# Linear attention and a top-2 mixture of experts on one core: fixed experts for each region's last rows, one plan for the rest, and output layers between the halves of the next first layers

## The chip, the cores and the metric

The kernel runs on one core of one Trainium2 chip. The metric is the device time of one execution in microseconds (us), without a profile; the median of three runs is taken. The kernel before took 337.9 us (337.5 to 340.69). A profile was recorded in a further execution.

## The reference

Two stages, each with a residual around it and a layer norm (without gain and bias) in front of it. B = 4 batches of 512 tokens of 256 numbers, all float32.

```python
# attention
q = k = x @ Wqk + bqk;  v = silu(x @ Wv + bv);  u = silu(x @ Wu + bu)
q = elu(heads(q)); kh = elu(heads(k)); vh = heads(v)      # 16 heads of 16
kv = einsum('bhnd,bhne->bhde', kh, vh)
out = einsum('bhnd,bhde->bhne', q, kv)
out = u * layernorm(out, ln_g, ln_b)
x = x + out @ Wo + bo
# experts: 8 of them, 256 -> 512 -> 256, the best two of each token
w, i = top_k(xn @ gate, 2); w = softmax(w)
h = silu(xn @ w0[e]) * (xn @ w1[e])
x = x + sum over the two of  w * (h @ wo[e])
```

The experts are computed here for the chosen tokens alone: 2048 tokens x 2 are 4096 rows, and each expert gets as many as chose it.

## The kernel before

**Rows by expert.** Each expert has a region of 2176 rows in a DRAM tensor xg. When a batch's gates are known, each token's two rows (the normed features, the weight and the token's number) are scattered into the regions of its two experts, behind the rows that are there already; POOL issues these scatters (L454). A block is 128 rows of one region, so one expert, and 32 to 39 blocks hold all rows, since a region's last block may be partly filled. Such a block's missing rows are written as padding (pads(), L462 to 469): rows of weight 0 with the numbers of spare tokens, 128 rows behind each region's end, eight DMAs of 130 KB on SP's queue.

**Planning.** Which regions the blocks lie in is known only at run time. plan(n, b) finds the first n blocks not yet taken: a matmul of ones with the counts (tot, L476) gives each region's end, some twenty small DVE operations on one partition (L483 to L539) turn this into a table with a first row and an expert's place in the weights for each block, and engines read the entries into registers (read(), L544). There are three plans: one for 9 blocks when the first two batches are scattered (EARLY), one for 16 more that are surely full when all four are (SURE - EARLY), and one for the last 14, of which 11 are usual (USUAL - SURE) and three come in a conditional part for unusual inputs. The last plan counts partly filled blocks too, and takes down where the padding starts.

**A block** goes through four steps, each in a function, and advance() moves a chain of blocks on by one step:
- fetch(): SP reads the first row and loads 128 rows of xg into g (L559; eight buffers, each free again when its block's add has landed).
- turn(): PE transposes g (gp, L570), ACT copies it out (L573), and ACT and DVE copy the expert's w0 and w1 (128x1024) from the resident weights to a staging place, found by the register (L579).
- hidden(): two times 16 matmuls, hp, one half for w0 and one for w1 (L590; each float32 matmul shows as two instructions), Silu of the first half on ACT (s, L596), the product on DVE (it, L598).
- finish(): four matmuls of it with the third weight (eo, L607), times the row's weight on DVE (ys, L612), and an indirect DMA on POOL that adds the rows to their tokens (L616).

The chain is such that PE's order is: transposes of block n+1, both halves of block n, eo of block n-1.

**Where the adds go.** The early blocks and those of the last plan add into a DRAM tensor y, which also has attention's result. The 16 surely full blocks are held back to the end: before their first add, y is copied to the output, and they add into the output. Adds into y are declared free of each other; adds into the output are not.

**Order.** Attention runs as four generators, one per batch, of 15 steps, started 4 steps apart; the loop's index is called at. The early plan is made at at = 19, the early blocks enter one per step from 20 on, so that the eighth enters at 27, the last index. Behind the loop come the two late plans, then the ninth early block, then the padding with the first block of the last plan, and the rest. This is the program's order; a planner in the compiler orders the instructions of each engine by it and by the times that it assumes, so that neighbours may be mixed. Each engine then executes in its own order. PSUM has eight buffers of one bank under one tag. In the page's names, blocks of the last plan end in r (g_0r, hp_0r); the names without r are early and held blocks.

Of the kernel before, what the change touches and what calls it, by code (L numbers as in the profile page):

```python
# [21 lines left out]
P = 128  # L22
# [7 lines left out]
def kernel(  # L30
# [35 lines left out]
    HPC = P // HEAD_DIM  # L66
    T = B * N
    TOPK = 2
    BLOCKS = T * TOPK // P + NE - 1
    USUAL = T * TOPK // P + NE // 2  # L70
    EARLY = 2 * N * TOPK // P - NE + 1
    SURE = T * TOPK // P - NE + 1
    REG = T + P
# [119 lines left out]
    ordinal = counting("ordinal", [1, BLOCKS, NE], [[1, BLOCKS], [0, NE]])  # L193
    rows = counting("rows", [1, BLOCKS], [[P, BLOCKS]])
# [3 lines left out]
    nc.gpsimd.memset(done, 0.0)  # L198
    empty = const.tile([P, ROW], F32, name="empty")
    nc.gpsimd.memset(empty, 0.0)  # L200
    nc.gpsimd.tensor_copy(empty[:, E + 1 : E + 2].bitcast(I32), spare_i)
# [255 lines left out]
                    bounds_check=NE * REG - 1, oob_is_err=True,  # L457
                ), b)

    def pads():  # L460

        loads, starts = nc.values_load_multi_w_load_instructions(  # L462
            state["pads"], engines=[mybir.EngineType.SP], min_val=0, max_val=NE * REG,
            skip_runtime_bounds_check_because="a region's start and a count",
        )
        for ins in loads:
            tc.keep_in_program_order(ins)
        for row in starts:
            apart(nc.sync.dma_start(out=xg[bass.ds(row, P), :], in_=empty), B - 1)

    def plan(n, b, last=False):

        tot = psum.tile([P, NE], F32, tag="a", name=f"tot_{b}_{last}")
        nc.tensor.matmul(tot, lhsT=ones, rhs=state["count"], start=True, stop=True)  # L476
        vec = [1, NE]

        def tmp(shape, what):
            return small.tile(shape, F32, tag=what, name=f"{what}_{b}_{last}", bufs=1)  # L480
# [13 lines left out]
        new = tmp(vec, "new")  # L494
        nc.vector.tensor_reduce(new, over, AX.X, ALU.add)
        nc.vector.tensor_tensor(new, new, done, ALU.subtract)
# [11 lines left out]
        nc.vector.tensor_tensor(base, done, cumex, ALU.subtract)  # L508
        nc.vector.scalar_tensor_tensor(base, base, float(P), region[0:1], ALU.mult, ALU.add)
# [19 lines left out]
        table = const.tile([1, 2, n], I32, name=f"table_{b}_{last}")  # L529
        nc.vector.tensor_scalar(table[:, 0, :], first, float(NE * REG), None, ALU.min)  # L530
        nc.vector.tensor_scalar(table[:, 1, :], which, float(NE - 1), float(OW), ALU.min, ALU.mult)
        if last:
            state["rest"] = const.tile([1, 1], I32, name="rest")
            nc.vector.tensor_copy(state["rest"], cum[:, NE - 1 : NE])
        else:
            taken = tmp(vec, "taken")
            nc.vector.tensor_scalar(taken, cumex, -1.0, float(n), ALU.mult, ALU.add)
            nc.vector.scalar_tensor_tensor(taken, taken, 0.0, new, ALU.max, ALU.min)
            nc.vector.tensor_tensor(done, done, taken, ALU.add)  # L539
        return [(f"{b}_{j}{'r' if last else ''}", b, table[0:1, :, j : j + 1]) for j in range(n)]  # L540

    def read(entry, most, *engines):

# [7 lines left out]

    def fetch(block):

        j, b, entry = block
        if j == f"{B - 1}_0r":
            pads()
        row = read(entry[:, 0, :], NE * REG, mybir.EngineType.SP)
        g = blk.tile([P, ROW], F32, tag="g", name=f"g_{j}", bufs=8)
        ins = nc.sync.dma_start(out=g, in_=xg[bass.ds(row, P), :])  # L559
        tc.declare_no_dep(ins.ins, group=f"after {b}", reason="rows of batches up to b")  # L560
        tc.add_to_no_dep_group("reads", ins.ins)
        return block, g

    def turn(block, g):


        j, b, entry = block
        ps = psum.tile([P, EC, P], F32, tag="a", name=f"gp_{j}")
        for c in range(EC):
            nc.tensor.transpose(ps[:, c, :], g[:, bass.ts(c, P)], ident)  # L570
# [3 lines left out]
        at = read(entry[:, 1, :], (NE - 1) * OW, mybir.EngineType.Activation, mybir.EngineType.DVE)  # L574
        w = []
        for i, copy in enumerate((nc.scalar.copy, nc.vector.tensor_copy)):
            w.append(staging[state["staged"] % 4])
            state["staged"] += 1
            copy(w[i], hw_sb[i][:, bass.ds(at, OW)])  # L579
        return block, w, g, gT  # L580

    def hidden(block, w, g, gT):

        j = block[0]
        both = []
        for i in range(2):
            ps = psum.tile([P, MC, P], F32, tag="a", name=f"hp_{j}_{i}")
            for m in range(MC):
                for k in range(EC):
                    nc.tensor.matmul(  # L590
                        ps[:, m, :], lhsT=w[i][:, bass.ds(k * M + m * P, P)],
                        rhs=gT[:, k, :], start=(k == 0), stop=(k == EC - 1),
                    )
            both.append(ps)
        s = work.tile([P, MC, P], F32, tag="s", name=f"s_{j}")
        nc.scalar.activation(s, both[0], AF.Silu)  # L596
        it = work.tile([P, MC, P], F32, tag="ex", name=f"it_{j}", bufs=4)
        nc.vector.tensor_tensor(it, s, both[1], ALU.mult)  # L598
        return block, g, it

    def finish(block, g, it):

        j, b, entry = block
        at = read(entry[:, 1, :], (NE - 1) * OW, mybir.EngineType.PE)
# [23 lines left out]
    def advance(block=None):  # L628
# [18 lines left out]
    for at in range(max(begin) + STAGES + 1):  # L647
# [4 lines left out]
            load_w2()  # L652

        if at == begin[1] + STAGES:
            ready += [None] * 1 + plan(EARLY, 1)
        if ready:
            block = ready.pop(0)
            if block:
                advance(block)

    held += plan(SURE - EARLY, B - 1)
    rest = plan(BLOCKS - SURE, B - 1, last=True)
    ready += rest[: USUAL - SURE]
    rare = rest[USUAL - SURE :]
    for block in ready + held:
        advance(block)
    while fetched or turned or made:
        advance()
    many = read(state["rest"], BLOCKS, *ENGINES)
    with tc.If(many > USUAL - (BLOCKS - len(rest))):  # L670
# [59 lines left out]
```

## Time and profile before

| what | us |
|---|---|
| median of three runs (lowest, highest) | 337.9 (337.5, 340.69) |
| the profiled execution, its own time | 345.68 |
| its span, first to last instruction | 343.6 |
| PE busy in the span | 305.5 |
| DVE, ACT, POOL busy | 162.7, 135.4, 118.4 |

The profile is of another execution than the three timed ones, and a longer one; a sum made from its rows belongs to its own 345.68 us. PE is TensorE's matmuls, PEld its weight loads, DVE the vector engine, ACT the scalar engine, POOL GpSimd, SP the engine whose queue loads most data. A line such as "PE hp L590 <- DVE arena L579: 2.0, 1, 2.0" says that PE, before an instruction of line 590 that writes hp, sat idle until DVE's line 579 was done, 2.0 us in all, one time, 2.0 us the longest. A timeline row gives the start, the duration, engine, line and operation, and in brackets the idle time of the engine before it. A "q" behind an engine (SPq) is its queue or sequencer.

Costs of single operations that the change touches:

| operation | duration of one, us | count |
|---|---|---|
| staging copy of w0 on ACT, L579 | 1.046 | 36 |
| staging copy of w1 on DVE, L579 | 0.693 | 36 |
| product it on DVE, L598 | 0.688 | 36 |
| Silu on ACT, L596 | 0.597 | 36 |
| ys on DVE, L612 | 0.482 | 36 |
| small operations of a plan on DVE | 0.13 to 0.28 | 20 each |
| add into the output on POOL, L616 | 1.602 | 16 |

### The profile page before, as it was taken

To read this page: it belongs to the slowest core of one execution; us is meant where nothing else is said; L and a number is where in the kernel's file an instruction comes from. 1 tells how busy PE (TensorE), PEld (TensorE's weight loads), DVE (VectorE), ACT (ScalarE), POOL (GpSimd) and SP (SyncE) were. 2 spreads that over 40 slices of the span, in tenths; PEclk is the share of its full clock that TensorE was granted. 3 is DMA by queue.
4 is the path that set the end of the run, shared out by engine and by line. 5 is a ranking of instruction groups with operands and counts; after the bars stand their busy time and mean duration, and the time that the engine had idled before them with its cause. 6 is when DMAs were issued, how large, how long until landed. Compare 5 with 4: busy or idle time off the path is not lost. (4 is left out here: it accounts for less than half of the span.)

```text
span 343.6 us, 6125 instructions
## 1 busy us (share of the span) xinstructions
PE 305.5 (89%) x2070; PEld 272.5 (79%) x2070; DVE 162.7 (47%) x556; ACT 135.4 (39%) x204; POOL 118.4 (34%) x147
## 2 busy tenths in 40 slices
PE   0999899899966898999789999999999999999950
PEld 0567686786866797998779999999999999999940
DVE  4756879686684764341823324232323324232210
ACT  1546728636524065531324243333424243333300
POOL 5420311317146076266324242333402333332321
PEclk9999999999995799999999999999999999999995
DMA  7999112044274542223552322323291433322121
GB/s 208 357 388 384 55 61 65 1 128 166 77 229 153 153 161 55 41 62 91 143 109 49 52 47 44 61 49 46 49 275 17 63 51 60 60 34 31 17 32 15
DMA packets 27871, 35.58 MB, mean 104 GB/s; under 512 B 2848, under 2 KB 22688, under 8 KB 27808
## 3 DMA queue, kind: packets, MB, share of 16 engines
q1 hardware_dynamic: 18960, 22.00, 20.4%
q0 software_dynamic: 6768, 11.08, 17.7%
q10 hardware_dynamic: 2112, 2.10, 1.9%
q8 instruction: 18, 0.29, 0.4%
q14 instruction: 13, 0.11, 0.1%
HBM read 22.89 MB, written 14.37 MB: 108 GB/s over the span
## 5 line engine op out<-in xcount | busy, mean ns | idle before, releaser
L590 PE MATMUL hp<-arena 128*128 128x128 f32 x800 | 94.5, 275 | 5.0 <-DVE arena L579 2.0
L590 PEld LDWEIGHTS hp<-arena 128*128 128x128 f32 x800 | 91.9, 192 | 5.7 <-issue 3.9
L598 DVE TENSOR_TENSOR it<-s,hp 128x512 f32<-128x512 f32 x25 | 17.2, 688 | 66.9 <-PE hp L590 51.1
L607 PE MATMUL eo<-arena,it 128*128 x200 | 47.5, 380 | 0.7 <-issue 0.7
L616 POOL DMA_INDIRECT out_dram<-ys,g x16 | 25.6, 1602 | 58.1 <-DVE ys L612 21.3
L454 POOL DMA_INDIRECT xg<-hn,idx_i x32 | 32.4, 1012 | 26.5 <-DVE mv L219 10.8
L607 PEld LDWEIGHTS eo<-arena,it 128*128 128x128 f32 x200 | 36.1, 190 | 5.0 <-issue 1.2
L579 ACT COPY arena<-w_sb 128x1024 f32 x36 | 37.6, 1046 | 4.0 <-DVE mv L219 1.3
L573 ACT COPY arena<-gp 128x256 f32<-128x256 f32 x25 | 9.3, 372 | 73.1 <-PE gp L570 65.7
L616 POOL DMA_INDIRECT y<-ys,g x9 | 15.3, 1702 | 29.9 <-DVE ys L612 13.8
L579 DVE COPY arena<-w_sb 128x1024 f32 x36 | 24.9, 693 | 1.3 <-DVE ys L612 0.7
L262 POOL TENSOR_TENSOR x<-x,bo 128x256 f32<-128x256 f32 x16 | 12.3, 794 | 37.7 <-DVE arena L245 29.1
L612 DVE TENSOR_SCALAR ys<-eo,g 128x256 f32<-128x256 f32 x25 | 12.0, 482 | 23.1 <-PE eo L607 20.6
L369 PE MATMUL ap<-wo,arena 128*128 128x256 f32 x64 | 17.2, 427 | 5.2 <-DVE first_False L526 2.8
L369 PEld LDWEIGHTS ap<-wo,arena 128*128 128x128 f32 x64 | 13.4, 216 | 8.3 <-issue 4.5
L596 ACT ACTIVATE s<-hp 128x512 f32<-128x512 f32 x25 | 14.9, 597 | 11.2 <-PE hp L590 9.5
L274 PE MATMUL qp<-arena,wqk 128*128 128x512 f32 x32 | 16.0, 647 | 0.2 <-ACT arena L267 0.2
L218 DVE BATCH_NORM_STATS2 st<-x 128x6 f32<-128x256 f32 x32 | 12.5, 416 | 4.5 <-DMA x<-in_x_dram 4.5
L292 PE MATMUL vp<-wv,arena 128*128 128x256 f32 x64 | 14.5, 379 | 0.0
L306 PE MATMUL up<-arena,wu 128*128 128x512 f32 x32 | 14.4, 592 | 0.0
L292 PEld LDWEIGHTS vp<-wv,arena 128*128 128x128 f32 x64 | 12.0, 190 | 2.4 <-issue 0.7
L253 PE MATMUL xTp<-ident,arena 128*128 128x128 f32 x32 | 5.2, 311 | 9.1 <-DVE arena L245 9.1
(269 smaller groups left out, 472.0 us busy)
## 6 DMA issues: line engine op xcount, KB each, us to landing
w_sb<-in_w_dram SPq DMA_DIRECT2D x16, 512.0 KB
arena<-in_w_dram SPq DMA_DIRECT2D x8, 512.0 KB
g<-xg SPq DMA_DIRECT2D x25, 130.0 KB
x<-in_x_dram SPq DMA_DIRECT2D x4, 512.0 KB
y<-x ACTq DMA_DIRECT2D x4, 512.0 KB
xg<-empty SPq DMA_DIRECT2D x9, 130.0 KB
xg<-hn,idx_i POOLq DMA_INDIRECT x32
wqk<-in_wqk_dram SPq DMA_DIRECT2D x1, 256.0 KB
```

Source lines behind the costliest of these rows:

```text
L218: nc.vector.bn_stats(out=st, in_=src[:, t, :])
L274: nc.tensor.matmul(ps, lhsT=wqk_sb[:, k, bass.ts(c, P)], rhs=xT[:, k, :], start=(k == 0), stop=(k == EC - 1),)
L292: nc.tensor.matmul(ps[:, t - t0, :], lhsT=xT[:, k, bass.ts(t, P)], rhs=wv_sb[:, k, :], start=(k == 0), stop=(k == EC - 1),)
L306: nc.tensor.matmul(ps, lhsT=wu_sb[:, k, bass.ts(c, P)], rhs=xT[:, k, :], start=(k == 0), stop=(k == EC - 1),)
L369: nc.tensor.matmul(ps[:, t - t0, :], lhsT=yT[:, c, bass.ts(t, P)], rhs=wo_sb[:, c, :], start=(c == 0), stop=(c == EC - 1),)
L454: apart(nc.gpsimd.indirect_dma_start(out=xg[:, :], out_offset=bass.IndirectOffsetOnAxis(ap=idx_i[:, t, k : k + 1], axis=0), in_=hn[:, t, k ...
L579: copy(w[i], hw_sb[i][:, bass.ds(at, OW)])
L590: nc.tensor.matmul(ps[:, m, :], lhsT=w[i][:, bass.ds(k * M + m * P, P)], rhs=gT[:, k, :], start=(k == 0), stop=(k == EC - 1),)
L596: nc.scalar.activation(s, both[0], AF.Silu)
L598: nc.vector.tensor_tensor(it, s, both[1], ALU.mult)
L607: nc.tensor.matmul(ps, lhsT=it[:, m, :], rhs=w2_sb[:, bass.ds(at + m * E, E)], start=(m == 0), stop=(m == MC - 1),)
L616: ins = nc.gpsimd.indirect_dma_start(out=whole[:, :] if full else y[:, :], out_offset=bass.IndirectOffsetOnAxis(ap=g[:, E + 1 : E + 2].bit ...
```

## The change

Number and order of blocks. The early plan of 9 stays. When all batches are scattered, the eight blocks with each region's last, partly filled rows are formed first: their experts are fixed (block last_e is expert e), so only the first row is found at run time, by a shift right and left by 7 of the region's end. One plan of 23 then finds the remaining full blocks, of which 19 are usual; 3 of these join the eight, and 16 are held back as before. The plan no longer counts partly filled blocks.

- total() makes the matmul tot once per plan stage; last_rows() needs two DVE operations. Both stand in the loop's last step, ahead of the eighth early block.
- pad() stands behind the ninth early block's fetch and ahead of the plan.
- Blocks with a fixed expert skip the staging copies: hp reads the resident weights at a fixed place, and eo its third weight too, without registers.
- hidden() is divided: advance() now does the first half and its Silu, then finish() of the block before, then the second half and the product. Also at the end of the chain.
- done is written by the early plan instead of being added to, so that the early plan has three operations less, and a memset goes.

```diff
-    BLOCKS = T * TOPK // P + NE - 1
-    USUAL = T * TOPK // P + NE // 2
+    FULL = T * TOPK // P
+    USUAL = FULL - NE // 2
...
+    def total():
+        tot = psum.tile([P, NE], F32, tag="a", name="tot")
+        nc.tensor.matmul(tot, lhsT=ones, rhs=state["count"], start=True, stop=True)
+        return tot
+    def last_rows(tot):
+        end = const.tile([1, NE], I32, name="end")
+        nc.vector.tensor_copy(end, tot[0:1, :])
+        first = const.tile([1, NE], I32, name="first")
+        nc.vector.tensor_scalar(
+            first, end, P.bit_length() - 1, P.bit_length() - 1,
+            ALU.arith_shift_right, ALU.logical_shift_left,
+        )
+        return [(f"last_{e}", B - 1, e, first[:, e : e + 1], None) for e in range(NE)], end
...
-    def plan(n, b, last=False):
+    def plan(tot, n, b, name):
...
-        if last:
-            state["pads"] = const.tile(vec, I32, name="pads_at")
-            nc.vector.tensor_copy(state["pads"], tot[0:1, :])
-            nc.vector.tensor_scalar(c, c, float(P - 1), None, ALU.add)
...
     def turn(block, g):
...
+        if e is not None:
+            return block, [sb[:, bass.ts(e, OW)] for sb in hw_sb], g, gT
...
     def finish(block, g, it):
...
+        if e is not None:
+            at = e * OW
+        else:
+            at = read(place, (NE - 1) * OW, mybir.EngineType.PE)
...
-        if turned and (len(turned) > 1 or not fetched):
-            made.append(hidden(*turned.pop(0)))
-        if made and (len(made) > 1 or not turned):
+        block = turned.pop(0) if turned and (len(turned) > 1 or not fetched) else None
+        if block:
+            s = work.tile([P, MC, P], F32, tag="s", name=f"s_{block[0][0]}")
+            nc.scalar.activation(s, half(0, *block), AF.Silu)
+        if made:
             finish(*made.pop(0))
+        if block:
+            made.append(hidden(s, *block))
...
+            ready += [None] * 1 + plan(total(), EARLY, 1, "early")
+        if at == begin[B - 1] + STAGES:
+            tot = total()
+            last, end = last_rows(tot)
         if ready:
             block = ready.pop(0)
             if block:
                 advance(block)
-    held += plan(SURE - EARLY, B - 1)
-    rest = plan(BLOCKS - SURE, B - 1, last=True)
-    ready += rest[: USUAL - SURE]
-    rare = rest[USUAL - SURE :]
-    for block in ready + held:
+    for block in ready:
+        advance(block)
+    pad(end)
+    blocks = plan(tot, FULL - EARLY, B - 1, "full")
+    held += blocks[: SURE - EARLY]
+    rare = blocks[USUAL - EARLY :]
+    for block in last + blocks[SURE - EARLY : USUAL - EARLY] + held:
         advance(block)
```

More of the change, by code (lines that the diff above doesn't have):

```diff
@@ L192 @@
     ends = counting("ends", [1, NE, T // P], [[0, NE], [P, T // P]], base=P)
-    ordinal = counting("ordinal", [1, BLOCKS, NE], [[1, BLOCKS], [0, NE]])
-    rows = counting("rows", [1, BLOCKS], [[P, BLOCKS]])
+    ordinal = counting("ordinal", [1, FULL, NE], [[1, FULL], [0, NE]])
+    rows = counting("rows", [1, FULL], [[P, FULL]])
     step = const.tile([1, NE], F32, name="step")
@@ L197 @@
     done = const.tile([1, NE], F32, name="done")
-    nc.gpsimd.memset(done, 0.0)
     empty = const.tile([P, ROW], F32, name="empty")
@@ L458, in attention, with pad @@
                 ), b)
-    def pads():
+    def total():
[11 more added lines that the diff above has]
+        return [(f"last_{e}", B - 1, e, first[:, e : e + 1], None) for e in range(NE)], end
+    def pad(end):
         loads, starts = nc.values_load_multi_w_load_instructions(
-            state["pads"], engines=[mybir.EngineType.SP], min_val=0, max_val=NE * REG,
+            end, engines=[mybir.EngineType.SP], min_val=0, max_val=NE * REG,
             skip_runtime_bounds_check_because="a region's start and a count",
@@ L469, in pads @@
             apart(nc.sync.dma_start(out=xg[bass.ds(row, P), :], in_=empty), B - 1)
-    def plan(n, b, last=False):
-        tot = psum.tile([P, NE], F32, tag="a", name=f"tot_{b}_{last}")
-        nc.tensor.matmul(tot, lhsT=ones, rhs=state["count"], start=True, stop=True)
+    def plan(tot, n, b, name):
         vec = [1, NE]
         def tmp(shape, what):
-            return small.tile(shape, F32, tag=what, name=f"{what}_{b}_{last}", bufs=1)
+            return small.tile(shape, F32, tag=what, name=f"{what}_{name}", bufs=1)
         c = tmp(vec, "c")
         nc.vector.tensor_tensor(c, tot[0:1, :], region[0:1], ALU.subtract)
-        if last:
-            state["pads"] = const.tile(vec, I32, name="pads_at")
-            nc.vector.tensor_copy(state["pads"], tot[0:1, :])
-            nc.vector.tensor_scalar(c, c, float(P - 1), None, ALU.add)
         full = [1, NE, T // P]
@@ L495, in plan @@
         nc.vector.tensor_reduce(new, over, AX.X, ALU.add)
-        nc.vector.tensor_tensor(new, new, done, ALU.subtract)
+        if b == B - 1:
+            nc.vector.tensor_tensor(new, new, done, ALU.subtract)
         sq = tmp([1, NE, NE], "sq")
@@ L507, in plan @@
         base = tmp(vec, "base")
-        nc.vector.tensor_tensor(base, done, cumex, ALU.subtract)
-        nc.vector.scalar_tensor_tensor(base, base, float(P), region[0:1], ALU.mult, ALU.add)
+        if b == B - 1:
+            nc.vector.tensor_tensor(base, done, cumex, ALU.subtract)
+            nc.vector.scalar_tensor_tensor(base, base, float(P), region[0:1], ALU.mult, ALU.add)
+        else:
+            nc.vector.scalar_tensor_tensor(base, cumex, -float(P), region[0:1], ALU.mult, ALU.add)
         nc.vector.tensor_tensor(
@@ L528, in plan @@
         )
-        table = const.tile([1, 2, n], I32, name=f"table_{b}_{last}")
+        table = const.tile([1, 2, n], I32, name=f"table_{name}")
         nc.vector.tensor_scalar(table[:, 0, :], first, float(NE * REG), None, ALU.min)
         nc.vector.tensor_scalar(table[:, 1, :], which, float(NE - 1), float(OW), ALU.min, ALU.mult)
-        if last:
-            state["rest"] = const.tile([1, 1], I32, name="rest")
-            nc.vector.tensor_copy(state["rest"], cum[:, NE - 1 : NE])
-        else:
[L536 to L540, printed above, removed]
+        if b == B - 1:
+            state["found"] = const.tile([1, 1], I32, name="found")
+            nc.vector.tensor_copy(state["found"], cum[:, NE - 1 : NE])
+        else:
+            nc.vector.tensor_scalar(done, cumex, -1.0, float(n), ALU.mult, ALU.add)
+            nc.vector.scalar_tensor_tensor(done, done, 0.0, new, ALU.max, ALU.min)
+        return [
+            (f"{name}_{j}", b, None, table[0:1, 0, j : j + 1], table[0:1, 1, j : j + 1])
+            for j in range(n)
+        ]
     def read(entry, most, *engines):
@@ L552, in fetch @@
     def fetch(block):
[L554 to L557, printed above, removed]
+        j, b, e, row, place = block
+        row = read(row, NE * REG, mybir.EngineType.SP)
         g = blk.tile([P, ROW], F32, tag="g", name=f"g_{j}", bufs=8)
@@ L564, in turn @@
     def turn(block, g):
-        j, b, entry = block
+        j, b, e, row, place = block
         ps = psum.tile([P, EC, P], F32, tag="a", name=f"gp_{j}")
@@ L573, in turn @@
         nc.scalar.copy(gT, ps)
-        at = read(entry[:, 1, :], (NE - 1) * OW, mybir.EngineType.Activation, mybir.EngineType.DVE)
+        if e is not None:
+            return block, [sb[:, bass.ts(e, OW)] for sb in hw_sb], g, gT
+        at = read(place, (NE - 1) * OW, mybir.EngineType.Activation, mybir.EngineType.DVE)
         w = []
@@ L580, in turn, with half, hidden @@
         return block, w, g, gT
[L582 to L598, printed above, removed]
+    def half(i, block, w, g, gT):
+        ps = psum.tile([P, MC, P], F32, tag="a", name=f"hp_{block[0]}_{i}")
+        for m in range(MC):
+            for k in range(EC):
+                nc.tensor.matmul(
+                    ps[:, m, :], lhsT=w[i][:, bass.ds(k * M + m * P, P)],
+                    rhs=gT[:, k, :], start=(k == 0), stop=(k == EC - 1),
+                )
+        return ps
+    def hidden(s, block, w, g, gT):
+        ps = half(1, block, w, g, gT)
+        it = work.tile([P, MC, P], F32, tag="ex", name=f"it_{block[0]}", bufs=4)
+        nc.vector.tensor_tensor(it, s, ps, ALU.mult)
         return block, g, it
     def finish(block, g, it):
-        j, b, entry = block
-        at = read(entry[:, 1, :], (NE - 1) * OW, mybir.EngineType.PE)
+        j, b, e, row, place = block
+        if e is not None:
+            at = e * OW
+        else:
+            at = read(place, (NE - 1) * OW, mybir.EngineType.PE)
         ps = psum.tile([P, E], F32, tag="a", name=f"eo_{j}")
@@ L654 @@
         if at == begin[1] + STAGES:
-            ready += [None] * 1 + plan(EARLY, 1)
+            ready += [None] * 1 + plan(total(), EARLY, 1, "early")
+        if at == begin[B - 1] + STAGES:
+            tot = total()
+            last, end = last_rows(tot)
         if ready:
@@ L668 @@
         advance()
-    many = read(state["rest"], BLOCKS, *ENGINES)
-    with tc.If(many > USUAL - (BLOCKS - len(rest))):
+    many = read(state["found"], FULL, *ENGINES)
+    with tc.If(many > USUAL - EARLY):
         zero = xpool.tile([P, NT, E], F32, tag="x", name="zero")
```

## The prediction

> **What bounds the kernel now.** I read first the page's busy shares, its 40 slices and its groups, then PE's waits, then three windows, then the timeline of those windows, last the chain of waits.
>
> ```profile
> PE 305.5 (89%) x2070; PEld 272.5 (79%) x2070; DVE 162.7 (47%) x556; ACT 135.4 (39%) x204; POOL 118.4 (34%) x147
> ...
> PE   0999899899966898999789999999999999999950
> ...
> PEclk9999999999995799999999999999999999999995
> ```
>
> PE is the bound, and the rest is at half or less. So only PE's holes and what follows PE can be saved. The holes are in slices 11 to 13 (about 95 to 120 us), in slice 19 (163 to 172 us), and at both ends. The windows give (columns: PE, PEld, DVE, ACT, POOL busy, PE clock, DMA share, GB/s):
>
> ```profile
> 158.10:180.20 22.10, 17.79 (x131) 16.41 (x130) 11.23 (x50) 5.83 (x9) 7.98 (x6) 1.00 0.54 118
> 180.20:323.80 143.60, 143.60 (x1094) 136.97 (x1093) 48.50 (x78) 52.42 (x78) 45.28 (x27) 1.00 0.34 60
> ```
>
> From 180.2 to 323.8 PE has no hole at all: 26 blocks in 143.6 us, 5.52 us each. One block is 0.21 us of transposes (gp), 3.58 us of hp (two halves of 1.79 us) and 1.73 us of eo. The stretch before it holds 22.10 - 17.79 = 4.31 us of holes, and PE's waits name them:
>
> ```profile
> PE hp L590 <- DVE arena L579: 2.0, 1, 2.0
> ...
> PE gp_0r L570 <- DMA g_0r<-xg: 1.5, 1, 1.5
> ```
>
> The third is 0.82 us "issue" at 161.7. There ACT, DVE and PE all resume together near 162.5 with no releaser on an engine, so I tie it to no edit. The timeline shows what the first two wait for:
>
> ```profile
> 164.72 4.00 SPq L469 DMA_DIRECT2D xg<-empty  x8
> ...
> 168.58 0.69 DVE L579 COPY arena<-w_sb 128x1024 f32 x1
> ...
> 170.85 0.16 DVE L530 TENSOR_SCALAR table_True<-first_True 1x14 int32<-1x14 f32 x1
> ...
> 171.95 0.35 SPq L559 DMA_DIRECT2D g_0r<-xg  x1
> ...
> 174.65 0.44 PE L570 MATMUL gp_0r<-ident,g_0r 128*128 128x128 f32 x2 [1.48 <-DMA g_0r<-xg]
> ```
>
> Both are the planning. The two tot matmuls run on PE at 158.1. DVE takes up the 40 operations of two plans at 162.94 and ends them at 171.0; the staging copy of the eighth early block stands among them. SP loads g_0r only when the second table exists, and the rows land 2.7 us after the issue.
>
> The chain of waits at the end:
>
> ```profile
> 330.03 1.54 DMA out_dram<-ys,g
> 331.57 2.77 issue
> 334.34 0.50 POOLq L544
> 334.85 1.25 POOL out_dram L616
> ```
>
> The adds into out are not exempted from each other, so the last waits until the one before has landed: 330.03 to 334.55, 4.52 us. ys of the last block was ready at 331.48. So **the end hangs on the last but one block's eo**, not on the last one's.
>
> **What the Trainium skill says.** "VectorE: DVE Perf Modes", § The TRN2 errata, gives (N+151)/0.96 ns for an fp32 tensor_tensor: 691 ns at N=512. The trace agrees: it<-s,hp 688 ns; the 128-element plan operations take 0.27 us against 0.29. It prices what the trace lacks, the 184-element operations of a plan of 23: 0.35 us. "DMA: Bandwidth & Descriptors", § Two DMAs through the same engine are not ordered, says that a dependent DMA must wait for the first one's completion semaphore; the 4.52 us between the two last adds fits that. "TensorE: Matmul & The Clock Gate", § HAM oscillation, warns of idle gaps over some 3.4 us halving the clock. Here the clock is 0.54 from 103.8 to 118.0, behind a hole of 3.04 us: lp<-gate x16 takes 3.64 us there, 1.85 elsewhere.
>
> **The change part by part.**
>
> (1) *Number of blocks*: 9 + 8 + 3 + 16 = 36 against 9 + 11 + 16 = 36. PE's matmuls stay but for one tot less: 0.
>
> (2) *Fixed experts*: eight blocks lose their staging copies, 8 x 1.05 us on ACT and 8 x 0.69 on DVE, and one register read on PE, ACT and DVE each. From 180.2 on PE never waits for these: 0.
>
> (3) *tot and last_rows ahead of the eighth early block*: tot moves one block forward in PE's queue, to about 152.6. Two DVE operations (0.15 us each) then give the row numbers, instead of a whole plan. A PSUM buffer of eight is held until the plan's first operation has read tot; a block in flight holds gp, two hp and eo at most, so 0.
>
> (4) *Padding*: the same eight DMAs of 130 KB move from 164.72 to about 153.5, behind the ninth row load (issued at 138.9) and ahead of g_last_0 on SP. They cost SP 4.0 us (to 157.5). Behind them wait only the loads of last_0 and on. Those also wait for batch 3's scatters, which POOL issues from 149.74 to 159.92; with some 2 us of landing, 162. The buffer that last_0 takes was freed by block 1's add, begun at 141.44. So the load is issued near 162 and lands 2.7 us later, near 164.7. PE asks for it at 158.47 + 2 x 5.52 = 169.5. Margin 4.8 us: **the 1.48 us go**. The padding now meets the scatters on the DMA engines (share 0.39 in 150 to 160); should that cost 2 us, the margin hides it.
>
> (5) *One plan behind the ninth block*: 40 operations become 20 (18 of the plan and the two above). The staging copies of blocks 7 and 8 now stand ahead of the plan or long before their use (block 8's is needed 5.5 us later than 7's). **The 2.01 us go.** What is late next is the plan itself: 18 operations, four of them 0.35 us, some 3.8 us of durations, 4.3 with the gaps of a dependent chain (layernorm's small operations start 0.20 us apart). Its table is first needed eight blocks, 44 us, later. The risk is DVE's order: put right before it of block 7, the plan would run 168.4 to 172.7, it would end at 173.4, and eo needs it at 171.5: a stall of 1.9 us. Put anywhere in the 5.5 us between two its behind the copy, it costs nothing. Bounds 0 and 1.9; I take 0, since its input is there from 153 on and DVE has a hole of 5.80 us up to 159.76.
>
> (6) *Early plan*: three DVE operations less, two of which stand between 109.8 and 111.3, ahead of the multiply that ap waits for: 2 x 0.08 = 0.15 us gained. Bounds 0 and 0.3.
>
> (7) *eo amid the next block's first layers*: PE's order becomes gp(n+1), half 0 of n, eo(n-1), half 1 of n. The cover of it(n-1) falls from 0.21 + 3.58 = 3.8 us to 0.21 + 1.79 = 2.0. Its lag is that of the trace: hp's last issue at 316.52, DVE's it from 316.79 to 317.48, seen by PE about 1.05 us after. A copy ahead of it makes 1.05 + 0.69 = 1.74, still under 2.0. Kinds of matmul follow each other now without a hole (32 x 0.112 = 3.58), so one more switch: 0. In the early blocks ACT's table load (1.28 us) makes it(0) end at 128.2 where eo(0) could start at 127.7: 0.5 us, in a place with 0.52 and 0.74 us of other holes. Bounds 0 and 1; I take 0.
> At the end: eo of the last but one ends 1.79 us earlier, so its add starts at 328.24 and lands at 332.56, and the last may start at 332.76. The last eo now waits openly for its own it: 1.05 us. It ends at 330.96 + 1.05 = 332.0, ys at 332.5, POOL at 332.8. Both paths meet at 332.8, against 334.55: **1.75 us gained**. The tail behind (9.0 us from 334.55 to the end of the span) stays.
>
> Sum: 1.48 + 2.01 + 0.15 + 1.75 = 5.4 us. The profiled execution took 345.68 us (span 343.6) and would take 340.3. It stands 7.8 us above the median of 337.9; some 5 of these are the slow clock at 104 to 118 us (lp 3.64 for 1.85, oTp 1.95 for 1.07, ap 5.97 for 3.72), which the change doesn't touch. Taken from the median: 337.9 - 5.4 = **332.5 us**. If the 0.82 goes too, 331.7.
>
> **Rivals.** *Gap refilled.* The plan or the padding moves the stall instead of removing it: the 1.9 us of (5) return, or the loads wait longer for scatters and padding that now run together. For it: DVE is in order and the copies already suffer from that. Against: margins of 4.8 and 2 us. 334.5 to 335.5.
> *It does not do what it says.* Instructions are ordered by the compiler's own planning, as DVE's mixed plans and layernorms show. If tot, row numbers or padding are issued where they were, the 3.5 us stay, and the tail alone counts: 336.1.
> *Slower: eo waits for it in every block.* From a lag of 2.0 us on, each block costs the excess, 35 times. Copy and one ys (0.48) ahead of it give 2.22 us, 0.22 x 35 = 7.7 us; three such operations give 0.4, 14 us. 340 to 346, and break-even at 0.15 us a block. For it: the cover is halved and DVE executes in order. Against: ys of n-1 cannot precede it of n-1, and DVE is only 34% busy in that stretch.
>
> **Numbers.** Forecast 0.62 (331 to 334), gap refilled 0.16, order unchanged 0.12, eo waits 0.10. Within 1% is what a measurement of this kernel cannot tell from no change, here 334.5 to 341.3. Faster 0.68 (the forecast and a part of the second), same 0.22, slower 0.10. The range goes from 330 (the 0.82, 0.3 early, and a little of the early holes) to 337, leaving out the last case and a run with the slow clock.
>
> **What would show it.** Right: no wait of gp for g_last and none of hp for L579 near 165 to 175; the padding near 154; PE full from about 146 on; the last two adds still some 4.5 us apart and POOL's last some 2 us after PE's end. Wrong: repeated waits of eo on it in the full stretch, a block period over 5.52 us, PE waiting for DVE's plan lines, or g_last_0 issued after 169.

## The result, and the profile after

| | before | after |
|---|---|---|
| median of 20 runs each | 337.87 us | 338.89 us |
| ratio after : before | | 1.0041 [1.0024, 1.0057] |
| profiled execution, time / span | 345.68 / 343.6 us | 338.75 / 337.0 us |

The change costs about 1 us, where a gain of 5.4 us was forecast. By the medians it is 1.0 us and by the ratio, which takes all runs, 1.4, because the times fall into two groups: 8 of the 20 runs after stand at 340.1 to 340.7 us with a granted clock of 0.959 (the others at 338.3 to 339.1 with 0.964 to 0.969), and only one of the 20 before at 340.7.

The two profiles say the opposite: the profiled execution of the kernel after is 6.9 us shorter than that of before. So either the two don't belong together, or a part of the time is not where I looked. Both turned out to be true.

The page of the kernel after, shares and slices:

```profile
PE 304.0 (90%) x2068; PEld 272.9 (81%) x2068; DVE 155.5 (46%) x525; ACT 126.6 (38%) x196; POOL 114.3 (34%) x146
...
PE   0999999899987879999999999999999999999930
...
PEclk9999999999996799999999999999999999999985
```

The hole in slice 19 is gone: counted from 0 as in the prediction, PE is full from slice 15 (126 us) to the end. The slow clock in slices 12 and 13 is still there. PE's waits (line waited for, us in total, times, longest), those at the blocks and the last attention step ahead of them:

```profile
PE hp_early L602 <- ACT arena L594: 1.7, 1, 1.7
PE ap L368 <- DVE chosen L417: 1.5, 1, 1.5
PE eo_full L624 <- DVE it_full L612: 0.9, 1, 0.9
...
PE eo_early L624 <- DVE it_early L612: 0.2, 1, 0.2
```

The signs that the prediction had named for being right are there: no wait for the plan's copies (L594 by DVE), none for g_last, the padding at 151.6 us. None of its signs for being wrong is. The padding on SP:

```profile
151.59 3.98 SPq L486 DMA_DIRECT2D xg<-empty  x8
```

The 0.9 us of eo_full is the last block's, which the prediction expected. The windows (columns as in the prediction):

```profile
120.00:150.00 30.00, 29.77 (x239) 28.75 (x238) 13.20 (x46) 15.41 (x22) 16.83 (x18) 1.00 0.28 71
150.00:182.00 32.00, 32.00 (x245) 30.76 (x244) 12.16 (x35) 8.93 (x15) 14.63 (x12) 1.00 0.50 110
182.00:320.00 138.00, 138.00 (x1053) 132.84 (x1052) 40.76 (x69) 43.74 (x68) 40.11 (x27) 1.00 0.35 60
```

PE has no hole from 150 to 320 us. The kernel before, in the same two first windows:

```profile
120.00:150.00 30.00, 27.51 (x219) 26.39 (x220) 14.16 (x52) 17.23 (x24) 15.27 (x16) 1.00 0.28 76
150.00:182.00 32.00, 27.69 (x206) 25.82 (x205) 14.28 (x55) 9.14 (x14) 15.07 (x13) 1.00 0.50 113
```

That is 6.8 us of holes against 0.2. The end (POOL's last two adds in the timeline of the kernel after):

```profile
319.77 1.54 POOL L633 DMA_INDIRECT out_dram<-ys_full,g_full  x1 [3.75 <-DVE ys_full L629]
324.40 1.54 POOL L633 DMA_INDIRECT out_dram<-ys_full,g_full  x1 [3.08 <-DVE ys_full L629]
```

The last add starts 0.8 us after the end of PE's last matmul (323.61); before it was 3.6 us (330.96 to 334.55). Part (7)'s sum has 0.8 too, the prediction's list of signs some 2. But from there to the end of the span it takes 337.0 - 324.4 = **12.6 us; before it took 343.6 - 334.55 = 9.1**. POOL's instructions in the raw records from the last add to the DRAIN, the last long one (start, duration, instruction, semaphores waited for; 111 to 118 are the eight semaphores of POOL's DMAs; a row that waits for another semaphore is left out):

```
before  334.55  1.54  DMA_INDIRECT out   its own: 115
        334.91  0.05  COMPARE_BRANCH
        ...
        335.21  0.04  EVENT_SEMAPHORE    116, 114
        335.30  0.04  EVENT_SEMAPHORE    117, 113
        335.39  0.04  EVENT_SEMAPHORE    118, 112
        335.48  1.58  INC_SWDGE_SEM      111
        337.09  5.71  DRAIN
after   324.40  1.54  DMA_INDIRECT out   its own: 115
        324.74  0.05  COMPARE_BRANCH
        ...
        328.18  0.02  EVENT_SEMAPHORE    115
        328.25  0.04  EVENT_SEMAPHORE    116, 114
        328.33  0.04  EVENT_SEMAPHORE    117, 113
        328.42  0.04  EVENT_SEMAPHORE    118, 112
        328.51  1.56  INC_SWDGE_SEM      111
        330.10  5.71  DRAIN
```

In the kernel after POOL waits for 115, the landing of the last add, before it begins the 1.6 and 5.7 us of closing. In the kernel before the closing starts while that add is in flight. "Perfetto Trace Analysis", § DMA Instruction — SWDGE (GPSIMD), in the Trainium skill says that such a DMA's row ends when its descriptors are written, not when the data are there. The trace agrees: the row is 1.54 us, and the wait for 115 ends 3.8 us after its start.

### The profile page after: what moved, and what is told of

Read it like the earlier page. It is cut to its first block, busy times and chain, and to the rows that moved or that the text cites. A ratio compares the mean times of both kernels' runs of the same rounds, so it can differ in the third digit from the quotient of the medians.

```text
span 337.0 us, 5947 instructions
## 1 busy us (share of the span) xinstructions
PE 304.0 (90%) x2068; PEld 272.9 (81%) x2068; DVE 155.5 (46%) x525; ACT 126.6 (38%) x196; POOL 114.3 (34%) x146
## 5 line engine op out<-in xcount | busy, mean ns | idle before, releaser
L602 PE MATMUL hp_full<-arena 128*128 128x128 f32 x608 | 73.9, 275 | 0.0
L602 PEld LDWEIGHTS hp_full<-arena 128*128 128x128 f32 x608 | 72.3, 192 | 1.0
L633 POOL DMA_INDIRECT out_dram<-ys_full,g_full x16 | 25.3, 1584 | 58.7 <-DVE ys_full L629 31.8
L624 PE MATMUL eo_full<-arena,it_full 128*128 x152 | 36.1, 380 | 0.9 <-DVE it_full L612 0.9
L602 PE MATMUL hp_early<-arena 128*128 128x128 f32 x288 | 35.0, 275 | 1.7 <-ACT arena L594 1.7
L602 PEld LDWEIGHTS hp_early<-arena 128*128 128x128 f32 x288 | 34.1, 192 | 2.3 <-ACT arena L594 1.9
L602 PE MATMUL hp_last<-arena,w_sb 128*128 128x128 f32 x256 | 31.2, 275 | 0.0
L602 PEld LDWEIGHTS hp_last<-arena,w_sb 128*128 128x128 f32 x256 | 30.5, 192 | 0.4
L624 PEld LDWEIGHTS eo_full<-arena,it_full 128*128 128x128 f32 x152 | 27.4, 190 | 4.0 <-DVE it_full L612 1.0
L594 ACT COPY arena<-w_sb 128x1024 f32 x28 | 29.3, 1047 | 3.5 <-DVE idx_i L439 1.5
L594 DVE COPY arena<-w_sb 128x1024 f32 x28 | 19.3, 690 | 1.3 <-issue 1.1
L624 PE MATMUL eo_early<-arena,it_early 128*128 x72 | 17.1, 381 | 0.2 <-DVE it_early L612 0.2
```

The source lines that it names most:

```text
L602: nc.tensor.matmul(ps[:, m, :], lhsT=w[i][:, bass.ds(k * M + m * P, P)], rhs=gT[:, k, :], start=(k == 0), stop=(k == EC - 1),)
L624: nc.tensor.matmul(ps, lhsT=it[:, m, :], rhs=w2_sb[:, bass.ds(at + m * E, E)], start=(m == 0), stop=(m == MC - 1),)
L633: ins = nc.gpsimd.indirect_dma_start(out=whole[:, :] if full else y[:, :], out_offset=bass.IndirectOffsetOnAxis(ap=g[:, E + 1 : E + 2].bit ...
```

## The experiments

In all, four chips served, one for each group of runs: A (the kernel before takes 337.6 us), B (344.9), C (347.5) and D (348.1). The chip of the result and of the profile before is not on record; the times of the result (337.87 us before) are those of chip A, and the profile's is like chip B's. Every ratio is to the kernel before on the same chip; a ratio in microseconds is taken of that chip's time before.

### Chip A: the slow clock and the two halves of the change

The first four expectations set two theories on the missing gain against each other: one holds the slow clock responsible ("clock theory"), the other what the two traces show at their holes and ends ("trace theory").

**e1, e2**: three matmuls with an unused result fill PE's hole of 3.04 us ahead of the slow clock, in the kernel before (e1) and after (e2).

```diff
             nc.scalar.copy(o[:, t0 : t0 + 2, :], ps)
+        if b == B - 1:
+            ps = psum.tile([P, N], F32, tag="a", name="warm")
+            for i in range(3):
+                nc.tensor.matmul(ps, lhsT=ident, rhs=kT[:, i % EC, :], start=True, stop=True)
```

> The kernel before, with three 128x512 matmuls whose result nobody reads put into PE's hole of 3.04 us at 99 us (about 2.7 us of work), so that the clock needn't fall. It leaves nothing out. Clock theory (the untraced runs of before keep the full clock at 104 to 118 us, those of the changed kernel lose it and give their gain back there): no difference to before, 337.4 to 338.4 us. Trace theory (the holes at 160 to 175 us that the change fills are those of a traced execution alone, and the clock falls untraced in both kernels alike): 333 to 335 us, by the 3 to 5 us of slow clock, and the same gain in the changed kernel.

> The changed kernel with the same three matmuls in the same hole. Clock theory: 333 to 334.5 us, 4 to 6 us under the changed kernel's 338.9, and without two groups of times. Trace theory: 334 to 336 us, as much gained as in the kernel before with the matmuls, so still equal to it within 1 us.

Measured: e1 334.41 us, 0.9900 [0.9869, 0.9931]; e2 336.36 us, 0.9941 [0.9921, 0.9960]. PE's timeline in e1:

```profile
98.89 2.74 PE L352 MATMUL warm<-arena,ident 128*128 128x512 f32 x6
...
103.44 2.22 PE L411 MATMUL lp<-gate,arena 128*128 128x8 f32 x16
```

The gates (lp) take 2.22 us instead of 3.64. Filling the hole gains 3.4 us in the kernel before and 2.5 in the kernel after (336.36 against 338.89). So the slow clock is in the timed runs of both kernels and doesn't tell them apart. e2 was expected within 1 us of e1 and stands 1.95 us above it: what the change loses lies elsewhere. The filling doesn't remove the slow clock: in e1 it is still 0.5 from 106.3 to 113.0 us. "TensorE: Matmul & The Clock Gate", § HAM oscillation, in the Trainium skill names idle gaps over some 3.4 us; here the slow stretch follows a hole of 3.04 us, and about half of it is left when that hole is filled (6.7 us in e1, 13.6 in the profile before, from 103.1 to 116.7). What brings on the rest is open.

**e3, e4**: the change in two. e3 is the kernel before with half(), hidden(s, ...) and advance() of the change alone (part 7); e4 is the changed kernel with hidden() and advance() of before (parts 1 to 6).

> The kernel before with the output layer put between the halves of the next first layer, and nothing else of the change. Clock theory: the tail's 1.75 us are gained, 336.1 us, if the clock stays as in before; about 341 if this edit is what makes it fall. Trace theory: 336.1 us. If the interleaving costs in every block: over 338.5 us.

> The changed kernel with the old order of hp and eo (both halves, then eo of the block before): fixed experts, early row numbers, early padding, one plan. Clock theory: with the clock as in before 334.2 us (3.6 less than before), with the clock fallen 339 to 340 us. Trace theory: 337.5 to 338.5 us, no gain, and then the changed kernel's 338.9 says that the halves cost something too.

Measured: e3 336.62 us, 0.9963 [0.9946, 0.9981], a gain of 1.2 us; e4 339.91 us, 1.0072 [1.0045, 1.0098], a loss of 2.4 us. By its time alone e4 would fit the clock theory with the clock fallen (339 to 340 us), but its clock fell no further than that of e3: from 95 to 120 us it is 0.80 in e4 and 0.73 in e3. The last two adds of e3:

```profile
321.53 1.54 POOL L615 DMA_INDIRECT out_dram<-ys,g  x1 [3.76 <-DVE ys L611]
326.15 1.54 POOL L615 DMA_INDIRECT out_dram<-ys,g  x1 [3.08 <-DVEq L673]
```

From the last add to the end of its span (335.2) there are 9.1 us; in e4 there are 12.6 (325.88 to 338.5). The longer closing belongs to the planning part, and outweighs it.

### Chip B: the closing, and the holes

What does the planning part do to POOL's closing? The part for unusual inputs behind tc.If is never entered here. In the kernel before it holds 39 - 36 = 3 blocks; after the change 23 - 19 = 4. Each block ends in an add on POOL, and four more adds bring y into out, so the skipped part has 7 DMAs on POOL in one case and 8 in the other. POOL's DMAs take the eight semaphores in turn: in both traces the last five adds have 111, 112, 113, 114 and 115, so that the DMAs of the skipped part would have 116, 117, 118, 111, 112, 113, 114, and an eighth 115 again. These are the semaphores that POOL waits for in the rows above before INC_SWDGE_SEM, an instruction that only stands where a part is skipped (e11, without the part, has none): seven in the kernel before, all eight in the kernel after. 115 is the last add's. The "closing theory" of the next expectations is this; the "outlier theory" says that the profiled execution of before has holes which its timed runs lack.

**e5** is the kernel before once more. **e6** is the changed kernel with one block less in the skipped part (it leaves out the case in which all 32 blocks are full ones), **e7** the kernel before with one more, **e8** is e4 with one less.

```diff
# e6, e8
-    blocks = plan(tot, FULL - EARLY, B - 1, "full")
+    blocks = plan(tot, FULL - EARLY - 1, B - 1, "full")
# e7
-    rest = plan(BLOCKS - SURE, B - 1, last=True)
+    rest = plan(BLOCKS - SURE + 1, B - 1, last=True)
...
-    with tc.If(many > USUAL - (BLOCKS - len(rest))):
+    with tc.If(many > USUAL - SURE):
```

> The kernel before, unchanged, profiled once more. Outlier theory (the holes of 4.31 us that the prediction counted at 158 to 180 us belong to the one execution shown, which took 345.68 us against a median of 337.9): about 338 us under the profile too, less than 1.5 us of PE holes there, the clock still halved at 104 to 118 us. Prediction's theory (the holes are there in every execution): again over 343 us, with holes of 4 us.

> The changed kernel with three instead of four blocks in the conditional part for unusual inputs, which this input never enters (the fourth, needed only where nearly every region is an exact multiple of 128 rows, is left out). Closing theory (the part has 4 adds and 4 accumulating DMAs, so that skipping it makes POOL account for all eight of its DMA semaphores, the last add's among them, and POOL waits for the landing before its closing 7.3 us): 335.8 us, 3.1 us under the changed kernel, and the wait gone from the end. Rival (the length or the place of the conditional code matters, as for instruction fetch): under 1 us gained. Rival (the loss is in the planning part earlier): no gain.

> The kernel before with one block more in the conditional part (four instead of three; never entered). Closing theory: 3.1 us slower than before, 340.7 us, with POOL's wait for the last landing at the end. Rivals: within 1 us of before.

> The changed kernel with the old order of hp and eo, and three blocks in the conditional part: the planning edits alone, without the eighth DMA. Closing theory with the outlier theory: 336.8 us, 0.8 to 1 us under before, the small holes that remain in a usual execution. Prediction's theory for the planning (3.6 us gained, the closing apart): 334.2 us.

Measured: e5 345.5 us; e6 0.9934 [0.9910, 0.9959]; e7 1.0089 [1.0055, 1.0122]; e8 0.9981 [0.9958, 1.0004]. The changed kernel itself wasn't run on this chip. One block that is never executed costs the kernel before 3.1 us [1.9, 4.2]. The instructions of the branch's line in e7 (on POOL: times, durations in ns, first and last start):

```profile
L670 POOLq EVENT_SEMAPHORE  x5: 17/43/43, 334.4 to 337.9; - x5
...
L670 POOLq INC_SWDGE_SEM  x1: 1564/1564/1564, 338.0 to 338.0; - x1
```

and in the kernel before:

```profile
L670 POOLq EVENT_SEMAPHORE  x4: 17/43/43, 335.1 to 335.4; - x4
...
L670 POOLq INC_SWDGE_SEM  x1: 1579/1579/1579, 335.5 to 335.5; - x1
```

Five waits over 3.5 us against four over 0.3: the closing theory holds in both directions, by adding the block to the one kernel and by taking it from the other (from the last add to the end of the span: 12.6 us in e7, 9.1 in e6 and e8).

e5 looks like the profile that the prediction was made from (span 343.6 too), so that execution was no outlier but is what the kernel does on such a chip (its 32 timed runs there are all between 342.6 and 348.0 us). Chip A's runs lack its holes. And e8, in which only the planning differs from before, gains 0.65 us on this chip (-0.1 to 1.45, so no gain is not ruled out), not 3.5.

### Chip C: a part that leaves the last add's semaphore alone

**e9** keeps all four blocks, but brings y into out with one DMA through free staging space in place of four; **e10** is e9 with the three matmuls of e2; **e11** is the changed kernel without the part for unusual inputs; **e12** is the kernel before with the one DMA.

```diff
-        for b in range(B):
-            extra = xpool.tile([P, NT, E], F32, tag="x", name=f"extra_{b}")
-            nc.sync.dma_start(out=extra, in_=y[b * N : (b + 1) * N, :].rearrange("(t p) e -> p t e", p=P))
-            nc.gpsimd.dma_start(
-                out=out[b].rearrange("(t p) e -> p t e", p=P), in_=extra, accum_op=ALU.add
-            )
+        extra = arena[:, 12:16, :].rearrange("p s (t e) -> p (s t) e", e=E)
+        nc.sync.dma_start(out=extra, in_=y[0:T, :].rearrange("(t p) e -> p t e", p=P))
+        nc.gpsimd.dma_start(
+            out=whole.rearrange("(t p) e -> p t e", p=P), in_=extra, accum_op=ALU.add
+        )
```

> The changed kernel with all four blocks in its part for unusual inputs, whose four adds of whole batches into out become one add of all of them. The part then has 5 DMAs on POOL instead of 8 and leaves the semaphore of the last add into out untouched. Semaphore-set theory (skipping the part makes POOL wait for the DMAs whose semaphores the part would have used): no wait for the last landing before the closing, 9.1 us from the start of the last add to the end of the span instead of 12.6, ratio to the kernel before 0.990 to 0.996. Size theory (a bigger skipped part costs by its blocks or its instructions): there are still four blocks, so 12.6 us stay and the ratio is near 1.004.

> The same with three matmuls of 128x512, whose result nobody reads, in PE's hole at 100 us (2.74 us of PE). If the two gains are independent: the closing 3.1 us and the clock 2.5 us below the changed kernel, ratio to the kernel before 0.983 to 0.988. If the earlier end is taken up by another wait: above 0.990.

> The changed kernel without the part for unusual inputs: it leaves out the blocks that only inputs with more full blocks need, and the branch to them. Semaphore-set theory: POOL has nothing to account for, so the 1.56 us of that instruction go as well as the wait, unless the closing itself then waits for the last landing. From the start of the last add to the end of the span: 7.5 us if the closing doesn't wait for the landing, 11 if it does. Ratio to the kernel before 0.986 to 0.990 in the first case, 0.997 to 1.001 in the second.

> The kernel before with the same one add in place of four. Its part already left the last add's semaphore untouched, so the semaphore-set theory expects no change: 9.1 us from the last add to the end, ratio 0.998 to 1.002. If fewer DMAs in the skipped part were worth something by themselves (some 0.8 us for each), the ratio would be 0.993 or less.

| run | ratio | last add to end of span |
|---|---|---|
| e9 | 0.9898 [0.9855, 0.9940] | 335.00 to 344.0: 9.0 us |
| e10 | 0.9943 [0.9905, 0.9980] | 335.36 to 344.3: 9.0 us |
| e11 | 0.9875 [0.9833, 0.9918] | 333.05 to 341.1: 8.1 us |
| e12 | 0.9990 [0.9963, 1.0018] | 336.99 to 346.0: 9.0 us |

e9 against the size theory: four blocks, and the 3.5 us (12.6 against 9.1 on chip A) are gone. In the raw records POOL waits there for five semaphores (116, 117, 118, 111, 112) where the skipped part has five DMAs, and in e12 for four (116, 117, 118, 111) where it has four: the set is the DMAs of the skipped part, counted on from the last add. e12 shows that fewer DMAs alone are worth nothing, as long as the last add's semaphore isn't among them. Without the part (e11) the closing is one DRAIN of 7.50 us instead of the 1.6 and 5.7, and 1 us shorter, between the two cases I had named.

e10 is a miss: what gave 1% on chip A gives nothing here. The timeline of e9 around PE's ap (start, us, engine, what, and the idle time before it with its releaser):

```profile
110.46 1.44 ACT L356 ACTIVATE arena<-oTp,cols 128x512 f32<-128x512 f32 x2 [4.38 <-PE oTp L252]
...
112.11 6.47 PE L368 MATMUL ap<-wo,arena 128*128 128x256 f32 x16 [2.46 <-DVE chosen L417]
```

The same of e10, with batch 1's last scatter:

```profile
107.23 0.97 POOL L457 DMA_INDIRECT xg<-hn,idx_i  x1 [0.30 <-issue]
...
109.94 1.45 ACT L360 ACTIVATE arena<-oTp,cols 128x512 f32<-128x512 f32 x2 [4.20 <-remote]
...
112.12 5.92 PE L372 MATMUL ap<-wo,arena 128*128 128x256 f32 x16 [5.54 <-DVE first_early L544]
```

PE had its transposes (oTp) done at 106.6 in e10 and at 109.7 in e9, but ACT resumes at 109.9 against 110.5, and ap begins at 112.1 in both. "remote" is a wait whose end the profile ties to no engine. Something other than the clock holds ACT and DVE there, and a batch's last scatter (107.23) stands 2.7 us ahead of ACT's resuming.

### Chip D: whose stall is it

The same picture stands at 160 us in every profile of chips B to D, and in that of the kernel before: ACT does nothing for 2.5 to 10 us and DVE little, PE has a hole or works off single instructions some 0.7 us apart, and all go on at nearly the same moment. The holes that the prediction meant to remove come right behind. This is called the stall below. **e13** is e9 once more, as a base. **e14** takes tot, the last rows and the padding back behind the early blocks. **e15** puts nine small copies on POOL ahead of batch 3's scatters, so that these run later.

```diff
# e14
-        if at == begin[B - 1] + STAGES:
-            tot = total()
-            last, end = last_rows(tot)
...
     for block in ready:
         advance(block)
+    tot = total()
+    last, end = last_rows(tot)
     pad(end)
# e15
+        if b == B - 1:
+            one = small.tile([P, E], I32, tag="one", name="one", bufs=1)
+            other = small.tile([P, E], I32, tag="other", name="other", bufs=1)
+            nc.gpsimd.memset(one, 0)
+            nc.gpsimd.tensor_copy(one[:, 0 : NT * TOPK], idx_i.rearrange("p t k -> p (t k)"))
+            for i in range(4):
+                nc.gpsimd.tensor_copy(other, one)
+                nc.gpsimd.tensor_copy(one, other)
+            idx_i = one[:, 0 : NT * TOPK].rearrange("p (t k) -> p t k", t=NT)
```

> e9's kernel once more, as the base of the next two. On a chip where PE has the stall near 160 us: PE's holes from 150 to 182 us some 2.5 to 3.5 us, ratio to the kernel before 0.990 to 0.996. On one without: PE full there, and the same ratio.

> e13's kernel with the counts' matmul (tot), the last rows and so the padding back behind the early blocks, as in the kernel before; the single plan stays. The prediction's steps on the padding: the wait of PE for g_last returns, 0.7 to 1.5 us, and DVE's plan again holds a staging copy, so +1.5 to +3.5 us over e13. Stall theory (the holes were the stall's consequence, not the late planning's): within 1 us of e13, and PE's holes in 150 to 182 us the same within 0.5 us.

> e13's kernel with nine small copies on POOL (some 3.3 us) ahead of batch 3's eight scatters, so that these run 3.3 us later. If the stall of all engines belongs to the scatters: it begins some 3.3 us later than in e13, and the time is up by at most 1 us. If it belongs to something else (a time, PE's or DVE's own work): it stays where it was in e13 within 1 us. On a chip without the stall this tells nothing.

Measured: e13 0.9882 [0.9838, 0.9926]; e14 1.0090 [1.0057, 1.0124]; e15 0.9973 [0.9951, 0.9995]. The timeline of e13, the last scatter and what resumes:

```profile
158.73 0.97 POOL L453 DMA_INDIRECT xg<-hn,idx_i  x1 [0.30 <-issue]
...
162.53 0.60 ACT L655 ACTIVATE s_early<-hp_early 128x512 f32<-128x512 f32 x1 [7.91 <-PE gp_early L583]
```

The same of e15:

```profile
162.66 0.98 POOL L462 DMA_INDIRECT xg<-hn,one  x1 [0.30 <-issue]
...
166.45 0.37 ACT L595 COPY arena<-gp_early 128x256 f32<-128x256 f32 x1 [9.70 <-remote]
...
167.22 3.78 PE L633 MATMUL eo_early<-arena,it_early 128*128 x8 [4.86 <-DVE it_early L621]
```

The scatters run 3.9 us later, and the end of the stall comes 3.9 us later: **the end of the stall follows batch 3's scatters**. ACT resumes 3.8 us after the last one's start in both. The beginning follows them less: PE's first gap comes at 158.5 us in e13 and at 160.2 in e15, where 3.3 us were expected. The add that POOL starts right behind the last scatter moved with it (160.01 and 163.95), so this pair alone doesn't tell the two apart; ahead of the wait at 110 us in e10 no add stands, only scatters. In the kernel before ACT resumes 3.7 us after the last scatter's start:

```profile
158.95 0.97 POOL L454 DMA_INDIRECT xg<-hn,idx_i  x1 [0.30 <-issue]
...
162.66 0.37 ACT L573 COPY arena<-gp 128x256 f32<-128x256 f32 x1 [7.28 <-remote]
```

e15's price, 3.1 us over e13, is above the 1 us that I had allowed: the stall is longer as well as later.

e14 costs 7.2 us over e13, outside both expectations. Its timeline:

```profile
168.35 0.29 PE L462 MATMUL tot<-count,ones 128*128 128x8 f32 x2
...
179.89 0.66 PE L583 MATMUL gp_last<-ident,g_last 128*128 128x128 f32 x2 [5.68 <-DMA g_last<-xg]
```

tot stands here 10 us later than in the kernel before (158.1), so e14 goes beyond undoing; it does show that the single plan without the early tot and padding doesn't keep PE from waiting for g_last.

## Why the prediction was wrong

**The step that failed** is the last sentence of part (7): "The tail behind (9.0 us from 334.55 to the end of the span) stays." It became 12.6 us. I had counted the blocks that are executed (36 = 36, part 1) and passed over the one more that is not. The profile before shows no such wait, since its skipped part leaves the last add's semaphore alone. e7 measures the wait at 3.1 us, and in e6 and e9 it is gone. Of the 6.4 to 6.8 us between forecast and measurement this is 3.1 to 3.5; some 2.8 are the planning, 0.5 the early blocks.

**Parts (4) and (5)**, 3.5 us, were mis-sized: their two waits go, as predicted, and the padding stands at 151.6 for about 153.5. But late planning alone costs little. On chip A e1 and e3 have the planning of the kernel before and no stall; in both PE doesn't wait for DVE's arena, and the one for g_0r is 0.24 and 0.56 us instead of 1.48. The windows of e1:

```profile
120.00:150.00 30.00, 30.00 (x240) 28.78 (x239) 13.01 (x38) 17.09 (x25) 18.71 (x19) 1.00 0.28 69
150.00:182.00 32.00, 31.76 (x241) 29.98 (x240) 16.16 (x58) 11.01 (x17) 12.37 (x10) 1.00 0.48 103
```

So the waits in the profile were mostly the rest of the stall, which the change doesn't touch: the plan's input was there at 158.6, and DVE took it up at 162.94, when the stall ended. What I noted as "0.82 us 'issue'" at 161.7, tied to no edit, was the stall itself, and the 2.01 and 1.48 were its echo. The planning part is worth 0.65 us on chip B (e8) and some 0.7 on chip A (e4's loss of 2.4 against the 3.1 of the closing), neither clear of zero. The profiles agree: between kernels of the same chip that differ in it, the first block behind the early ones starts at most 2.2 us earlier with the new planning, and once 0.5 later (chip A: 163.87 in e1, 164.37 in e2, and 168.00 in e3; chip B: 174.69 in e5, 172.62 in e8; chip C: 177.11 in e12, 176.90 in e9, 174.95 in e11). The stall is also what the rival "gap refilled" lacked: in e13 PE's holes in 150 to 182 us are 2.8 us, and the clock is slow behind them:

```profile
150.00:182.00 32.00, 29.20 (x196) 27.04 (x195) 10.53 (x33) 6.87 (x12) 15.58 (x13) 0.89 0.46 109
```

**"Some 5 of these are the slow clock"** was wrong. The slow clock is in all runs (0.960 to 0.971 over the whole of chip A's runs of before, 0.968 in the profiled execution); most of the 7.8 us between the profiled execution and the median are holes (6.8 us from 120 to 182 us, against 0.2 in e1 and 1.2 in e3). Subtracting a gain seen in one execution from the median of others was the second error of size.

**Part (7)**, 1.75 us: the mechanism was right, and the size at the end exact. From the transposes of the first block behind the early ones to the last add it takes 159.9 us in the kernel before and in e1, 158.15 in e3 and 158.1 in the kernel after: 1.75 less. With the old order it stays at 160.3 in e4 and 160.1 in e8. Of this e3 keeps 1.2 [0.6, 1.8]; the early eo's wait for it (0.2 to 1.1 us in the profiles), which I bounded by 0 and 1 and took as 0, fits the rest. The last eo waits 0.9 us for its it, 1.05 predicted. The block period stays at 5.52 us, no eo waits in the full stretch: the rival "slower" didn't happen, and the slower end came from elsewhere.

**Parts (1), (2), (3)** cost nothing that shows, and (6), 0.15 us, is below what can be seen.

The two halves of the change add up on chip A: -1.2 us (e3) and +2.4 (e4, the closing included) make +1.2 us; the whole measured +1.4 [0.8, 1.9] by the ratio.

**What beats both kernels**: e9, the change with one add of y in place of four, measured twice: 0.9898 [0.9855, 0.9940] on chip C and 0.9882 [0.9838, 0.9926] on chip D. The second lies a little beyond the 0.990 to 0.996 that were expected. That is 3.5 and 4.1 us, more than the halves (1.2 to 1.75 us) and the planning of e8 (0.65) give together; whether the planning is worth more on these chips or this is noise is open. On a chip like A it wasn't tried; e6, which ends in the same way, gained 0.66% on chip B.

**Open**: why scatters stall the other engines on chips B to D and not on A, and through what. That the stall's end moves with them is shown; the mechanism is not.

## What to carry to other kernels

Count what a branch holds also where it is never taken: if its DMAs on POOL use the semaphore of the last store ahead of it, skipping it waits for that store's landing, and the whole closing moves behind it. Signs of being right have to cover the whole span: here nearly all came true, and the loss stood behind the last of them. Before a hole is priced by the wait that ends it, look whether all engines resume at the same moment; then the wait may be an echo, and removing its named cause lets the next one stand there. A profile and a median from different chips can't be subtracted from each other.

## What was not expected of the hardware

- Skipping a part of the program with DMAs on POOL made POOL wait for exactly the DMA semaphores that the part would have used: 4, 5, 7 or 8 of them with as many DMAs (e12, e9, before, after). The one more that was the last add's cost 3.1 us (e7).
- The closing on POOL is 1.56 us (INC_SWDGE_SEM, there only where a part with DMAs is skipped) and 5.71 us (DRAIN); it runs beside the landing of the last add unless something makes it wait.
- The same program took 337.6, 344.9, 347.5 and 348.1 us on four chips, and on three of them ACT resumed 3.6 to 4.1 us after the start of batch 3's last scatter, whatever the kernel.
- POOL goes on through that stall: in e13 the last scatter and the add behind it start 1.28 us apart, as the scatters ahead of them do. SP's eight padding DMAs take 8.7 us there, 4.0 in the kernel after, whose profile has no stall.
